# Last cross-attention of a decoder: exponentials meet context rows with a column of ones instead of projected values

## The chip, the cores and the metric

The kernel runs on one core of one Trainium2 chip, as one program. The time is device microseconds of one execution; lower is better. All arithmetic of the part discussed here is in float32.

## The reference

The program is a decoder of four layers, each with a self-attention, a cross-attention to a context of 1601 rows and a feed-forward part. After each part the input is added and a layer norm follows. x has the shape (4, 256, 128), the context (4, 1601, 96). The change concerns the last cross-attention alone:

```
def _L3_xattn_ref(x, context, Wq, Wk, Wv, Wo, bo):   # 16 heads of 64
    q = (x @ Wq).reshape(b, n, h, d).transpose(0, 2, 1, 3)
    k = (context @ Wk).reshape(b, -1, h, d).transpose(0, 2, 1, 3)
    v = (context @ Wv).reshape(b, -1, h, d).transpose(0, 2, 1, 3)
    sim = jnp.einsum('bhid,bhjd->bhij', q, k) * scale
    attn = jax.nn.softmax(sim, axis=-1)
    out = jnp.einsum('bhij,bhjd->bhid', attn, v)
    out = out.transpose(0, 2, 1, 3).reshape(b, n, h * d)
    return out @ Wo + bo
```

What follows it is a layer norm, an int8 feed-forward part and a last layer norm.

## The kernel before

The function `l3_xattn` (from line 1852) works through 32 units: a batch row b of 4 and a pair of heads hp of 8. The 1601 context rows of a unit are cut into 13 chunks of 128 rows (the last has 65), and these are worked on in four steps: four chunks in each of the first three, one in the fourth. The two heads of a pair lie in the two halves of 64 partitions. Scores are held transposed: context rows on the partitions, the 256 queries of each head along the free dimension. A tile `St` holds two chunks of both heads (128 x 1024).

TensorE (PE), VectorE (DVE) and ScalarE (ACT) each do their instructions in the order in which the code writes them (`manual_schedule`, line 2047); SyncE's loads and GpSimd's few instructions are placed by the framework. The loop at line 2048 counts steps g and writes for each:

- `running(g-1)` (DVE): the running maximum over the copied scores, L1937 and L1940; at a unit's end L1944 folds it to `mx`. For the first two steps of a unit's four it stands at the loop's top, for the others after the maxima.
- `spread` (PE, then an ACT copy to `Mb`, L1968): brings a unit's maxima to all partitions. Once per unit, where g % 4 is 1.
- `shifted(gb)` (DVE, L1974): subtracts the maxima from `St`. gb is g - 5: this half of the pipeline runs five steps, a little over a unit, behind the scores.
- `queries` (PE, DVE copy), once per unit, where g % 4 is 3.
- `projections(g+1, gb)`: PE makes the keys of step g+1 and the values of step gb in one PSUM tile of the pool `big`; ACT copies both halves out (L1918).
- `weights(gb)` (ACT, L1981): exponentials in place in `St`.
- `advance(later)`: lets deferred work take one step. Among it is `ended(u)`, which finishes a unit: two products spread the row sums, DVE takes the reciprocal (L2022) and multiplies (L2025).
- `sums(gb-1)` (PE): exponentials times values, and exponentials times a block of ones for the row sums, accumulated in one PSUM tile `acc` of the pool `one` over the unit's four steps. After the fourth, ACT copies the row sums to `rows` (L2013), and `ended` is put off to the next step.
- `maxima` (PE, DVE reduction L1956), once per unit, where g % 4 is 0.
- `scores(g)` (PE; ACT copies to `St`, L1930).

Values are projected per chunk with the context as stationary operand:

```
self.mm(ps[d, 512 + c * P : 512 + (c + 1) * P],
        self.ctx_all[:CD, o + d.start : o + d.stop], wv[:, hp * P : (hp + 1) * P])
```

An instruction of PE issued by the helper `mm` carries line 388 whatever it does, so the rows are told apart by their tiles. In the profile `big<-ctx,w` is the key projection, `big<-w,ctx` the value projection, `big<-Q,K` the scores, `one<-St,V` exponentials with values, `one<-St,c` exponentials with ones, `one<-rows,c` the products in `ended`, `one<-c,mx` the maxima and `one<-c,mq` the spread. A float32 product shows as two records. The shapes after a name are contraction rows x columns of the stationary operand, then rows x columns of the moving one.

PSUM has three tiles of the pool `big` (1024 columns) and two of the pool `one` (512 columns) in this stage. `acc` holds one of the two `one` tiles for most of a unit; queries, maxima and spread share the other.

Below, the four steps of a unit in the steady state are called A (g % 4 = 1, with the spread), B (2, with `ended` of the unit whose last chunk was summed in A), C (3, with the queries) and D (0, with the maxima).

Of the kernel before, what the change touches and what calls it, by code (L numbers as in the profile page):

```python
# [21 lines left out]
B, T, D = 4, 256, 128  # L22
P = 128
# [21 lines left out]
SW = 32  # L45
# [229 lines left out]
def _host(w):  # L275

    packs = {"c": _constants(), "p0": _pack0(w), "p1": _pack1(w), "p2": _pack2(w)}
    for i in range(NL):
        packs[f"p3_{i}"] = _pack3(w, i)
    packs["al"] = _alibi()  # L280
    packs["p4"], packs["p5"] = _pack4(w), _pack5(w)
    up, gp, down = Pack(NE * FM), Pack(NE * FM), Pack(sum(map(len, MOE_IN)) * D)
    up.add("w", w["L2_ffn_up_w"].transpose(2, 0, 1).reshape(D, NE * FM))
    gp.add("w", w["L2_ffn_gp_w"].transpose(2, 0, 1).reshape(D, NE * FM))
    dw = w["L2_ffn_down_w"].transpose(0, 2, 1)
    parts = []
    for e in range(NE):
        for i in MOE_IN[e]:
            parts.append(np.zeros((P, D), np.float32))
            lo, hi = max(MOE[i][0], e * FM), min(MOE[i][1], (e + 1) * FM)  # L290
            parts[-1][lo - MOE[i][0] : hi - MOE[i][0]] = dw[e, lo - e * FM : hi - e * FM]
    down.add("w", np.concatenate(parts, 1))
    packs.update(up=up, gp=gp, down=down)
    arrays = {n: c.a for n, c in packs.items()}
    ctx = w["ctx_768"].transpose(2, 0, 1).reshape(CD, B * S2)
    arrays["ctx"] = np.ascontiguousarray(ctx)
    arrays["x"] = np.ascontiguousarray(w["x"])
    arrays["mask"] = np.ascontiguousarray(w["mask_BxS2_bf1"]).view(np.uint8)
    arrays["wq8"] = np.ascontiguousarray(w["L3_ffn_weight_q"].T).view(np.int32)
    return arrays, {n: c.at for n, c in packs.items()}  # L300


class Net:
# [1548 lines left out]
    def l3_xattn(self):  # L1852
# [2 lines left out]

        nc = self.nc
        HD, LAG = 64, 5
        halves = [slice(0, HD), slice(HD, P)]  # L1860
        wq, wk, wv = self.w("p4", "Wq"), self.w("p4", "Wk", CD), self.w("p4", "Wv", CD)
        units = [(b, hp) for b in range(B) for hp in range(NH // 2)]
        steps = 4 * len(units)
        qs, ks, vs, sts, mx, top, accs, outs = {}, {}, {}, {}, {}, {}, {}, {}
        later = [self.in_turn(self.taken_over())]
        w8 = self.tile("w8", [P, D // 4], I32, pool=self.const)
        nc.sync.dma_start(w8, self.dram["wq8"])
# [3 lines left out]
        one = [kept[:, i].rearrange("p (n d) -> p n d", n=NB) for i in range(8, 11)]  # L1871
        places = {"h": kept[:, 4:8], "x1": one[0], "x3": one[1], "xn": one[2]}
        self.late = places.get

        def parts(g):

# [9 lines left out]
            qs[u] = self.tile("Q", [P, T], bufs=2)  # L1886
            nc.vector.tensor_copy(qs[u], ps[:, :T])

        def projections(gk, gv):

            ps, copies = self.big(), []
            if 0 <= gk < steps:
                b, hp = units[gk // 4]
                lo = gk % 4 * 4 * P
                n = min(4 * P, S2 - lo)
                for d in halves:
                    cols = slice(hp * P + d.start, hp * P + d.stop)
                    self.mm(ps[d, :n], wk[:, cols], self.ctx[:CD, b, lo : lo + n])
                ks[gk] = self.tile("K", [P, 4 * P], bufs=2)
                copies.append((ks[gk][:, :n], ps[:, :n]))  # L1900
            if 0 <= gv < steps:
                b, hp = units[gv // 4]
                lo = b * S2 + gv % 4 * 4 * P
                n = min(4, NCH - gv % 4 * 4)
                for c in range(n):
                    o = lo + c * P
                    for d in halves:
                        self.mm(
                            ps[d, 512 + c * P : 512 + (c + 1) * P],
                            self.ctx_all[:CD, o + d.start : o + d.stop],  # L1910
                            wv[:, hp * P : (hp + 1) * P],
                        )
                vs[gv] = self.tile("V", [P, 4, P], bufs=3)
                copies.append(
                    (vs[gv][:, :n, :].rearrange("p c d -> p (c d)"), ps[:, 512 : 512 + n * P])
                )
            for to, at in copies:
                nc.scalar.copy(to, at)  # L1918

        def scores(g):  # L1920
            u = g // 4
# [10 lines left out]
        def running(g):  # L1932
            u = g // 4
            for k, nc_, kp in parts(g):
                if k == 1:
                    mx[u] = kept[:, :4].rearrange("p (h c) t -> p h c t", h=2)
                    nc.vector.tensor_max(mx[u], sts[u, 0], sts[u, 1])  # L1937
                elif k:
                    to = mx[u][:kp, :, :nc_, :]
                    nc.vector.tensor_max(to, to, sts[u, k][:kp, :, :nc_, :])  # L1940
            if g % 4 == 3:
                m = mx.pop(u)
                mx[u] = self.tile("mx", [P, 2, T], bufs=2)
                nc.vector.tensor_max(mx[u], m[:, :, 0, :], m[:, :, 1, :])  # L1944

        def maxima(u):
# [11 lines left out]
        def spread(u):  # L1958

            ps, m = self.misc(), mx.pop(u)  # L1960
            for j in range(2 * NB):
                for d in halves:
                    self.mm(
                        ps[d, j * P : (j + 1) * P],
                        m[:, j : j + 1].broadcast_to([P, HD]), self.ident,
                    )
            top[u] = self.tile("Mb", [P, 2, T], bufs=2)
            nc.scalar.copy(top[u].rearrange("p h t -> p (h t)"), ps)  # L1968

        def shifted(g):  # L1970
# [12 lines left out]
        def sums(g):  # L1983
            u = g // 4
            if g % 4 == 0:
                accs[u] = self.misc()
            acc = accs[u]
            es = [(k, nc_, sts.pop((u, k))[:kp]) for k, nc_, kp in parts(g)]
            for k, nc_, e in es:
                for c in range(nc_):  # L1990
                    i = 2 * k + c
                    for h, d in enumerate(halves):
                        if i < NCH - 1:
                            self.mm(
                                acc[d, :T], vs[g][:, i - g % 4 * 4, d], e[:, h, c, :],
                                start=i == 0, stop=False,
                            )
            for k, nc_, e in es:
                kp = e.shape[0]
                for c in range(nc_):  # L2000
                    for h in range(2):
                        d = slice(HD * h + SW * c, HD * h + SW * c + SW)
                        self.mm(
                            acc[d, T:], self.w("c", "ones", kp)[:, :SW], e[:, h, c, :],
                            start=False, stop=False,
                        )
                if kp < P:
                    for h, d in enumerate(halves):
                        self.mm(acc[d, :T], vs[g][:kp, 0, d], e[:, h, 0, :], start=False)
            vs.pop(g)  # L2010
            if g % 4 == 3:
                rows = self.tile("rows", [P, T], bufs=1)
                nc.scalar.copy(rows, acc[:, T:])  # L2013
                later.append(ended(u, rows))

        def ended(u, rows):
            b, hp = units[u]
            acc = accs.pop(u)
            for d in halves:
                self.mm(acc[d, T:], self.w("c", "both")[:, d], rows)  # L2020
            rec = self.tile("rec64", [P, T])
            nc.vector.reciprocal(rec, acc[:, T:])  # L2022
            if hp == 0:
                outs[b] = self.tile(f"w{SLOT['p3_2']}", [P, NH // 2, T], pool=self.wpool)
# [20 lines left out]

        engines = {nc.tensor.engine, nc.vector.engine, nc.scalar.engine}
        with self.tc.manual_schedule(engines=engines):
            for g in range(-1, steps + LAG + 2):
                gb = g - LAG
                if g % 4 < 2 and 0 <= g - 1 < steps:  # L2050
                    running(g - 1)
                if g % 4 == 1 and 4 < g <= steps + 1:
                    spread(g // 4 - 1)
                if 0 <= gb < steps:
                    shifted(gb)
                if 0 <= g + 1 < steps and (g + 1) % 4 == 0:
                    queries((g + 1) // 4)
                if g + 1 < steps or gb < steps:
                    projections(g + 1, gb)
                if 0 <= gb < steps:  # L2060
                    weights(gb)
                self.advance(later)
                if 0 <= gb - 1 < steps:
                    sums(gb - 1)
                if g % 4 == 0 and 4 <= g <= steps:
                    maxima(g // 4 - 1)
                if g % 4 > 1 and 0 <= g - 1 < steps:
                    running(g - 1)
                if 0 <= g < steps:
                    scores(g)  # L2070
            while later:
                self.advance(later)
# [59 lines left out]
```

## Time and profile before

| | |
|---|---|
| Median of 3 runs | 2832.32 us (2829.03 to 2837.85) |
| Profiled execution | 2829.03 us, span 2827.2 us |
| PE busy | 2696.4 us (95% of the span) |
| PE weight loads busy | 1776.1 us (63%) |
| DVE busy | 1803.9 us (64%) |
| ACT busy | 1533.0 us (54%) |
| GpSimd (POOL) busy | 178.4 us (6%) |
| Mean granted clock of PE | 0.983 |
| The last attention with what follows | from 1957 to 2827.2 us, PE busy 845.91 of 870.20 us |

Engines have a queue each and wait for one another by semaphores. Time is in microseconds from the span's start; a timeline row gives the start, the length from the first start to the last end of a merged group, the engine, the line, the operation, the tiles written and read, the shapes and the number of records; a bracket holds the idle time ahead of it and who ended it. Matmuls overlap, so what one group costs is read from its start to the next group's start. Short idle times of the weight loader marked "issue" are not waits for another engine.

### The profile page before, as it was taken

Reading aid. Unit: us, or ns where it says so; the run is one execution under the profiler, and the core shown is the slowest. Engines: PE = TensorE matmul, PEld = TensorE weight load, DVE = VectorE, ACT = ScalarE, POOL = GpSimd, SP = SyncE. Lnnn points to the kernel's source line nnn. Section 1 sums busy time; section 2 is a strip of 40 time slices with the busy share of each in tenths; the row PEclk is TensorE's granted clock in tenths of the full one; section 3 lists DMA queues with packets and bytes.
Section 4 is the critical chain, followed back from the end, with each engine's and each line's share of the span. In section 5 each row is a group of like instructions: output and inputs, shape, how many; then the busy total and the mean of one; then the engine's idle time right before and its main releaser. Section 6 shows DMA issues by size and latency. Waiting matters only on the chain.

```text
span 2827.2 us, 62963 instructions
## 1 busy us (share of the span) xinstructions
PE 2696.4 (95%) x27003; PEld 1776.1 (63%) x27003; DVE 1803.9 (64%) x3946; ACT 1533.0 (54%) x2943; POOL 178.4 (6%) x191
## 2 busy tenths in 40 slices
PE   7999999898889999999999999998999999999997
PEld 4555565566655555555897777776656666666664
DVE  6656666364567665664455766665757777777775
ACT  2555555455534555555553444445656666666564
POOL 2000110110010000000001111101100000000000
PEclk9999999999989999999999999999999999999999
DMA  3000000000020000000002000000000000000000
GB/s 114 1 2 1 2 1 2 1 1 1 1 79 23 1 2 1 1 2 1 1 1 103 2 14 2 2 2 2 2 1 2 3 2 2 3 1 2 3 1 3
DMA packets 5223, 27.65 MB, mean 10 GB/s; under 512 B 584, under 2 KB 2764, under 8 KB 3408
## 3 DMA queue, kind: packets, MB, share of 16 engines
q1 hardware_dynamic: 4944, 23.62, 2.4%
q8 instruction: 212, 3.47, 0.5%
q14 instruction: 67, 0.55, 0.1%
HBM read 23.07 MB, written 0.52 MB: 8 GB/s over the span
## 4 chain that ended last, share of the span: by engine, by line
PE 87%; DVE 8%; ACT 2%; issue 1%; DMA 0%; POOL 0%; POOLq 0%; ACTq 0%; DVEq 0%; SPq 0%
PE one L388 63%; PE big L388 13%; PE acc L388 8%; DVE M L898 1%; PE one L533 1%; PE one L824 1%; PE one L461 1%; DVE St L1974 1%; DVE mpad L686 1%; DVE Ms L681 1%; ACT w L1313 0%; ACT E L720 0%; PE one L1323 0%; DVE w L1940 0%; DVE ln_st L475 0%
## 5 line engine op out<-in xcount | busy, mean ns | idle before, releaser
L898 DVE TENSOR_REDUCE M<-one 128x1 f32<-128x458 f32 (+3 forms) x1024 | 528.7, 568 | 292.2 <-PE one L388 291.0
L921 ACT ACTIVATE E<-one 128x512 f32<-128x512 f32 (+1 forms) x896 | 457.8, 563 | 424.0 <-PE one L388 423.7
L388 PE MATMUL one<-Q,K 32*128 32x256 f32 (+1 forms) x3328 | 532.8, 403 | 1.5 <-DVE M L898 1.5
L388 PE MATMUL one<-K,Q 32*128 32x458 f32 (+3 forms) x2048 | 459.2, 541 | 1.6 <-DVE M L898 1.6
L388 PEld LDWEIGHTS one<-Q,K 32*128 32x128 f32 (+1 forms) x3328 | 311.1, 180 | 62.4 <-DVE M L898 35.6
L1930 ACT COPY St<-big 128x1024 f32<-128x1024 f32 (+1 forms) x224 | 204.3, 959 | 159.8 <-PE big L388 159.8
L388 PEld LDWEIGHTS one<-K,Q 32*128 32x128 f32 x2048 | 171.3, 185 | 142.9 <-issue 79.9
L1974 DVE TENSOR_TENSOR St<-St,Mb 128x1024 f32<-128x1024 f32 (+1 forms) x224 | 245.3, 1142 | 1.8 <-ACT Mb L1968 1.8
L388 PE MATMUL acc<-E,V 128*32 128x256 f32 (+1 forms) x3328 | 234.1, 388 | 7.1 <-ACT E L921 7.1
L720 ACT ACTIVATE E<-one 128x384 f32<-128x384 f32 (+1 forms) x352 | 154.3, 525 | 143.9 <-PE one L388 143.7
L1981 ACT ACTIVATE St<-St 128x1024 f32<-128x1024 f32 (+1 forms) x224 | 215.1, 1014 | 25.4 <-DVE St L1974 25.3
L388 PE MATMUL big<-Q,K 64*128 64x256 f32 (+1 forms) x1664 | 214.4, 393 | 0.0
L388 PE MATMUL one<-St,V 128*64 128x256 f32 (+1 forms) x1664 | 204.1, 382 | 0.4
L481 POOL TENSOR_TENSOR ln_r<-ln_ve,half 128x2 f32<-128x2 f32 x92 | 71.0, 771 | 2104.5 <-DVE ln_ve L479 2047.0
L1940 DVE TENSOR_TENSOR w<-w,St 128x1024 f32<-128x1024 f32 (+1 forms) x160 | 178.7, 1117 | 34.7 <-ACT St L1930 27.5
L388 PE MATMUL one<-xT,w 128*128 128x256 f32 (+1 forms) x664 | 169.7, 396 | 18.6 <-DVE Q L1116 8.3
L681 DVE TENSOR_REDUCE Ms<-one 128x3 f32<-128x384 f32 x256 | 130.4, 552 | 84.8 <-PE one L388 84.6
L388 PEld LDWEIGHTS big<-Q,K 64*128 64x128 f32 (+1 forms) x1664 | 147.7, 183 | 57.4 <-issue 40.2
L388 PEld LDWEIGHTS acc<-E,V 128*32 128x32 f32 (+1 forms) x3328 | 87.5, 109 | 125.6 <-issue 70.8
L388 PEld LDWEIGHTS one<-St,V 128*64 128x64 f32 (+1 forms) x1664 | 113.5, 137 | 62.7 <-issue 14.6
L388 PEld LDWEIGHTS big<-w,ctx 96*64 96x64 f32 x1664 | 97.1, 137 | 54.0 <-issue 53.9
L388 PEld LDWEIGHTS one<-xT,w 128*128 128x128 f32 (+1 forms) x664 | 96.5, 180 | 49.5 <-issue 15.6
(308 smaller groups left out, 3978.0 us busy)
## 6 DMA issues: line engine op xcount, KB each, us to landing
w<-in_p SPq DMA_DIRECT2D x4, 1483.0 KB, 10.3
ctx<-in_ctx SPq DMA_DIRECT2D x4, 600.4 KB, 13.5
w<-in_down SPq DMA_DIRECT2D x1, 2112.0 KB
w<-in_up SPq DMA_DIRECT2D x1, 1632.0 KB, 6.3
w<-in_gp SPq DMA_DIRECT2D x1, 1632.0 KB
w<-in_p SPq DMA_DIRECT2D x1, 1536.0 KB, 15.1
w<-in_p SPq DMA_DIRECT2D x1, 1413.0 KB, 12.2
w<-in_p SPq DMA_DIRECT2D x1, 1382.0 KB
```

The costliest lines, as they stand in the source:

```text
L388: self.nc.tensor.matmul(out, lhsT, rhs, start=start, stop=stop)
L461: self.nc.tensor.transpose(ps[:, n * P : (n + 1) * P], x[:, n, :], self.ident)
L481: nc.gpsimd.tensor_tensor(rstd, ve, self.half[:, :NB], ALU.pow)
L533: self.nc.tensor.transpose(ps[:rows, n * P : (n + 1) * P], m4[:, n, :rows], self.ident)
L681: nc.vector.reduce_max(out=m[:, j, :], in_=ps[:, : 3 * P].rearrange("p (s c) -> p s c", c=P), axis=AX.X,)
L720: nc.scalar.activation(es[t, j], ps[:, :w], AF.Exp, scale=scale)
L898: nc.vector.reduce_max(out=ms[i][:, n, j, part : part + 1], in_=ps[:, at : at + hi - lo], axis=AX.X)
L921: nc.scalar.activation(e[:kp, :w], ps[:kp, :w], AF.Exp, scale=scale)
L1930: nc.scalar.copy(st[:kp, :, :nc_, :], ps[:kp, :, :nc_, :])
L1940: nc.vector.tensor_max(to, to, sts[u, k][:kp, :, :nc_, :])
L1974: nc.vector.tensor_sub(e, e, top[u][:kp].unsqueeze(2).broadcast_to([kp, 2, nc_, T]))
L1981: nc.scalar.activation(e, e, AF.Exp, scale=HD**-0.5)
```

## The change

The values are no longer projected. Each head's output is exp(S) (C Wv) / sum; the changed kernel computes (exp(S) C) Wv / sum.

- The host lays out the context rows a second time, with chunk rows on the partitions, padded to 13 chunks and with a 97th column of ones: the input `ctx_rows`. `context_rows(b)` loads one batch row of it (128 x 1261 float32, two buffers): b = 0 ahead of the loop, each further one in the step where g % 32 is 16.
- `projections` becomes `keys`: only the key projection and its one ACT copy are left.
- `sums` makes one product per chunk: the stationary operand is the chunk's 97 columns of context and ones, the moving operand the exponentials of both heads (512 columns), accumulated to a 97 x 512 tile. Rows 0 to 95 hold exp(S) C, row 96 the row sums. After the fourth step ACT copies all of it to `met`, where it copied 256 columns of row sums to `rows`.
- `ended` takes a second PSUM tile of the pool `one`: two products of the value weights of each head with `met` give the numerators, two of `last` (97 x 64, zeros but for ones in the last row) with `met` spread the row sums; reciprocal and multiplication stay.
- `mx`, `Mb` and `rec64` get one buffer instead of two. `last` is filled by two memsets of GpSimd.

```diff
+        def context_rows(b):
+            rows[b] = self.tile("rows", [P, NCH, CR], bufs=2)
+            n = NCH * CR
+            nc.sync.dma_start(
+                rows[b].rearrange("p c d -> p (c d)"),
+                self.dram["ctx_rows"][:, b * n : (b + 1) * n],
+            )
...
-        def projections(gk, gv):
...
+        def keys(g):
+            ps = self.big()
+            b, hp = units[g // 4]
+            lo = g % 4 * 4 * P
+            n = min(4 * P, S2 - lo)
+            for d in halves:
+                cols = slice(hp * P + d.start, hp * P + d.stop)
+                self.mm(ps[d, :n], wk[:, cols], self.ctx[:CD, b, lo : lo + n])
+            ks[g] = self.tile("K", [P, 4 * P], bufs=2)
+            nc.scalar.copy(ks[g][:, :n], ps[:, :n])
...
             if g % 4 == 0:
-                accs[u] = self.misc()
-            acc = accs[u]
...
+                accs[u] = self.misc()[:CR]
+            acc = accs[u].rearrange("p (h t) -> p h t", h=2)
+            for k, nc_, kp in parts(g):
+                e = sts.pop((u, k))
                 for c in range(nc_):
                     i = 2 * k + c
...
+                    self.mm(
+                        acc, rows[units[u][0]][:kp, i, :], e[:kp, :, c, :],
+                        start=i == 0, stop=i == NCH - 1,
+                    )
...
             if g % 4 == 3:
-                rows = self.tile("rows", [P, T], bufs=1)
-                nc.scalar.copy(rows, acc[:, T:])
-                later.append(ended(u, rows))
+                met = self.tile("met", [CR, 2, T], bufs=1)
+                nc.scalar.copy(met.rearrange("p h t -> p (h t)"), accs.pop(u))
+                later.append(ended(u, met))
...
-            acc = accs.pop(u)
-            for d in halves:
-                self.mm(acc[d, T:], self.w("c", "both")[:, d], rows)
+            acc = self.misc()
+            for h, d in enumerate(halves):
+                self.mm(acc[d, :T], wv[:, hp * P + d.start : hp * P + d.stop], met[:CD, h, :])
+            for h, d in enumerate(halves):
+                self.mm(acc[d, T:], last, met[:, h, :])
...
-                if g + 1 < steps or gb < steps:
-                    projections(g + 1, gb)
+                if 0 <= g + 1 < steps:
+                    keys(g + 1)
+                if g % 32 == 16 and 1 <= g // 32 + 1 < B:
+                    context_rows(g // 32 + 1)
```

More of the change, by code (lines that the diff above doesn't have):

```diff
@@ L296, in _host @@
     arrays["ctx"] = np.ascontiguousarray(ctx)
+    rows = np.zeros((B, NCH * P, CD + 1), np.float32)
+    rows[:, :S2, :CD] = w["ctx_768"]
+    rows[:, :S2, CD] = 1.0
+    rows = rows.reshape(B, NCH, P, CD + 1).transpose(2, 0, 1, 3)
+    arrays["ctx_rows"] = np.ascontiguousarray(rows.reshape(P, B * NCH * (CD + 1)))
     arrays["x"] = np.ascontiguousarray(w["x"])
@@ L1859, in l3_xattn @@
         HD, LAG = 64, 5
+        CR = CD + 1
         halves = [slice(0, HD), slice(HD, P)]
@@ L1863, in l3_xattn @@
         steps = 4 * len(units)
-        qs, ks, vs, sts, mx, top, accs, outs = {}, {}, {}, {}, {}, {}, {}, {}
+        qs, ks, rows, sts, mx, top, accs, outs = {}, {}, {}, {}, {}, {}, {}, {}
         later = [self.in_turn(self.taken_over())]
@@ L1873, in l3_xattn @@
         self.late = places.get
+        last = self.tile("last", [CR, HD], bufs=1)
+        nc.gpsimd.memset(last, 0.0)
+        nc.gpsimd.memset(last[CD:], 1.0)
+        def context_rows(b):
[5 more added lines that the diff above has]
+            )
         def parts(g):
@@ L1887, in queries @@
             nc.vector.tensor_copy(qs[u], ps[:, :T])
-        def projections(gk, gv):
[L1891 to L1895, printed above, removed]
-                for d in halves:
[L1897 to L1918, printed above, removed]
+        def keys(g):
[8 more added lines that the diff above has]
+            nc.scalar.copy(ks[g][:, :n], ps[:, :n])
         def scores(g):
@@ L1942, in running @@
                 m = mx.pop(u)
-                mx[u] = self.tile("mx", [P, 2, T], bufs=2)
+                mx[u] = self.tile("mx", [P, 2, T], bufs=1)
                 nc.vector.tensor_max(mx[u], m[:, :, 0, :], m[:, :, 1, :])
@@ L1966, in spread @@
                     )
-            top[u] = self.tile("Mb", [P, 2, T], bufs=2)
+            top[u] = self.tile("Mb", [P, 2, T], bufs=1)
             nc.scalar.copy(top[u].rearrange("p h t -> p (h t)"), ps)
@@ L1985, in sums @@
             if g % 4 == 0:
-                accs[u] = self.misc()
-            acc = accs[u]
-            es = [(k, nc_, sts.pop((u, k))[:kp]) for k, nc_, kp in parts(g)]
-            for k, nc_, e in es:
+                accs[u] = self.misc()[:CR]
+            acc = accs[u].rearrange("p (h t) -> p h t", h=2)
+            for k, nc_, kp in parts(g):
+                e = sts.pop((u, k))
                 for c in range(nc_):
                     i = 2 * k + c
[L1992 to L2009, printed above, removed]
@@ L2010, in sums @@
-            vs.pop(g)
+                    self.mm(
+                        acc, rows[units[u][0]][:kp, i, :], e[:kp, :, c, :],
+                        start=i == 0, stop=i == NCH - 1,
+                    )
             if g % 4 == 3:
-                rows = self.tile("rows", [P, T], bufs=1)
-                nc.scalar.copy(rows, acc[:, T:])
-                later.append(ended(u, rows))
-        def ended(u, rows):
+                met = self.tile("met", [CR, 2, T], bufs=1)
+                nc.scalar.copy(met.rearrange("p h t -> p (h t)"), accs.pop(u))
@@ L2017, in ended @@
+                later.append(ended(u, met))
+        def ended(u, met):
             b, hp = units[u]
-            acc = accs.pop(u)
-            for d in halves:
-                self.mm(acc[d, T:], self.w("c", "both")[:, d], rows)
-            rec = self.tile("rec64", [P, T])
+            acc = self.misc()
[3 more added lines that the diff above has]
+                self.mm(acc[d, T:], last, met[:, h, :])
+            rec = self.tile("rec64", [P, T], bufs=1)
@@ L2047, in l3_xattn @@
         with self.tc.manual_schedule(engines=engines):
+            context_rows(0)
             for g in range(-1, steps + LAG + 2):
```

## The prediction

> **What bounds the kernel now.** The change touches only the last attention, so I read the page's chain first, then busy time by stretch inside that stage, then the timeline of one unit (one batch row, two heads).
>
> ```profile
> PE 87%; DVE 8%; ACT 2%; issue 1%; DMA 0%; POOL 0%; POOLq 0%; ACTq 0%; DVEq 0%; SPq 0%
> ```
>
> ```profile
> 2300.00:2400.00 100.00, 100.00 (x1080) 63.02 (x1078) 71.77 (x72) 69.08 (x98) 0.00 (x0) 1.00 0.01 1
> ```
>
> The chain runs over PE, and in these 100 us PE is never idle at a granted clock of 1.00, while DVE (72) and ACT (69) have room. So a unit costs what PE's order of work costs, start to start. That is read from the timeline (start, length, engine, line); starts matter, lengths overlap:
>
> ```profile
> 2300.52 1.09 PE L388 MATMUL one<-c,mq 128*64 128x128 f32 x16
> ...
> 2301.79 1.23 DVE L1937 TENSOR_TENSOR w<-St,St 128x1024 f32<-128x1024 f32 x1 [2.38 <-ACT St L1930]
> ...
> 2302.93 4.62 DVE L1974 TENSOR_TENSOR St<-St,Mb 128x1024 f32<-128x1024 f32 x4
> ...
> 2304.42 2.00 PE L388 MATMUL big<-Q,K 64*128 64x256 f32 x16
> 2306.32 0.37 ACT L2013 COPY rows<-one 128x256 f32<-128x256 f32 x1
> ...
> 2306.34 0.34 PE L388 MATMUL big<-ctx,w 96*64 96x65 f32 x4
> ...
> 2306.51 1.04 PE L388 MATMUL big<-w,ctx 96*64 96x128 f32 x16
> ...
> 2307.39 0.60 PE L388 MATMUL one<-rows,c 128*64 128x256 f32 x4
> ...
> 2307.82 1.90 PE L388 MATMUL one<-St,V 128*64 128x256 f32 x16
> ...
> 2309.65 1.07 PE L388 MATMUL one<-St,c 128*32 128x256 f32 x16
> ...
> 2310.65 2.00 PE L388 MATMUL big<-Q,K 64*128 64x256 f32 x16
> ```
>
> The next unit's `c,mq` begins at 2325.11, so a unit is 24.59 us. Its four steps start at 2300.52, 2306.34, 2312.57 and 2318.20: A (spread) 5.82, B (`ended`) 6.23, C (queries) 5.63, D (maxima) 6.91. Note `rows`: ACT copies it at 2306.32, done by 2306.69; PE asks for it only at 2307.39, because 16 value-projection records lie ahead. At the end of the kernel, with less PE work ahead, the same place does stall (1.54 us, last line):
>
> ```profile
> 2787.78 4.63 DVE L1974 TENSOR_TENSOR St<-St,Mb 128x1024 f32<-128x1024 f32 x4 [1.81 <-ACT Mb L1968]
> ...
> 2791.14 0.35 ACT L2013 COPY rows<-one 128x256 f32<-128x256 f32 x1
> ...
> 2791.55 0.65 PE L388 MATMUL one<-rows,c 128*64 128x256 f32 x4 [1.54 <-ACT rows L2013]
> ```
>
> **PE work removed, per unit** (start to start). Value projections .97+.88+.87+.22 = 2.94. Exponentials with V: 3x1.83, and .58 for the 65-row chunk, 6.07. Row sums by ones: 3x1.00+.56 = 3.56. The two `both` products .43. Together 13.00. A float32 product is two records.
>
> **PE work added.** 13 products of 97 columns over 512 moving columns, and two pairs in `ended`. No row has this shape exactly; the nearest is a full-width product with 512 moving columns in an earlier stage:
>
> ```profile
> 616.01 1.02 PE L388 MATMUL one<-ctx,w 97*128 97x512 f32 x2
> 616.87 1.05 PE L388 MATMUL one<-w,ctx 97*128 97x128 f32 x8
> ```
>
> One product takes .86 start to start, so 13 are 11.1. The pairs, two halves side by side like `both`, are .43 each: .86. Bare sum 11.98 against 13.00: one microsecond gained. The 13 give no gain by themselves: V work ran two products side by side (8 in 1.83) and ones four (8 in 1.00), and a 97-column product has no neighbour. Bounds: .85 each (two in 1.71 at 626.34) up to 1.0, if operand strides between the heads cost something; I take .86.
>
> **Switches of shape.** The removed figures already contain what is lost between groups of different shape; the new .86 doesn't. The start of this stage shows full-width products among half-width ones:
>
> ```profile
> 1957.79 1.06 PE L388 MATMUL big<-ctx,w 96*64 96x512 f32 x4
> 1958.78 0.44 PE L461 MATMUL one<-c,heads 128*128 128x128 f32 x2
> 1959.14 1.08 PE L388 MATMUL big<-ctx,w 96*64 96x512 f32 x4
> 1960.15 0.71 PE L388 MATMUL one<-w,oT 128*128 128x128 f32 x4
> 1960.80 1.57 PE L388 MATMUL big<-Q,K 64*128 64x256 f32 x12
> ```
>
> Keys into full width: .99 and 1.01 where keys followed by value projections take .86, so +.15. Full width into scores: .65 for 4 records of 128 columns that need .43, so +.21. The Trainium skill ("TensorEngine Tiling (Array Packing)", Key Properties) says that changing the tiling mode, not just the tile, drains the engine. Counting modes by that rule, B and C keep three switches, D four and A goes from four to three: by the rule's count the drains nearly cancel and about 1 us per unit stays won. The rows differ: V to ones lost .12 and ones to scores .15, while the new pair costs .15+.21. I take the rows, which decide.
>
> So, without waits: A: spread .93, keys 1.01, one product .86+.21, scores 1.92 = 4.93. B: keys .17, `ended` .86+.13, four products 3.42+.21, scores 1.92 = 6.71. C: queries .49, keys 1.01, 3.63, scores .58 = 5.71. D: keys 1.01, 3.62, maxima 1.02, scores 1.93 = 7.58. Sum 24.93 against 24.59: +.34 per unit before any wait.
>
> **The wait that appears.** Now `ended` needs `met`, a copy of the accumulator by ACT, queued behind two exponentials of the same step. Those follow DVE: scores of D, their copies, L1937, then the subtractions L1974. None of this chain is shortened. ACT loses its V copy ahead of the exponentials (.60), but the first must then wait for the first subtraction and the second for the second. The stage's end shows that case: first subtraction 2787.78 to `both` 2791.55 is 3.77 us. `met` (97x512) costs .59 by the 128x512 row of `Mb` (.586) instead of .35, so 4.01. In the steady unit the subtraction starts 2.41 after the spread (2302.93-2300.52), so `ended` starts at 6.42. PE arrives at 4.93+.17 = 5.10 and waits 1.32. Behind it on PE queue the step's four products and scores B; ACT's copies and DVE's maxima wait for those. In exchange nothing comes earlier: the loop's start is scores of D, which move with PE. New period: 6.42 + .99+3.63+1.92 (rest of B) + 5.71 + 7.58 = 26.25, or +1.66 per unit.
>
> **What is covered.** ACT is relieved of 2.07 us of V copies a unit and pays .22 for `met`; it is not the bound, so nothing is gained. `mx`, `Mb`, `rec64` with one buffer: each is last read over 5 us before its rewrite a unit later. Four DMAs of 646 KB (128 x 1261 x 4 bytes; 13.5 us to land for `ctx`, 600 KB): the first is needed six steps in, some 25 us later, the others about 16 steps after issue; SP has only outputs to pass. Were the first late, PE would wait at most those 13.5 us once. The two POOL memsets are needed some 45 us in, after queued POOL work of .7 to 1.6 us a piece. Extra PSUM tile in `ended`: freed after the multiplication (2309.90+.42 = 9.8 after the spread), wanted by queries at 6.42+.99+3.63+1.92 = 12.96; cost nothing, up to 1 us if that cover went.
>
> **Sum.** 30 units have both the wait and followers: 30x1.66 = 49.8. The first units carry leftover work of the stage before, which fills some wait: about -3 (estimate: one step of .4 to 2 us in each of four units). The first unit has no `ended`: -.3. At the end the last `met` comes about 1.4 later (2803.31 to 2804.75 by the same durations). Together +48 on the profiled execution's 2829.0, its span 2827.2 and 1.8 around it: 2877. The median stands 3.3 above that execution; I forecast 2878, 1.6% slower.
>
> **Rivals.** (1) Wait without switch costs: .86 everywhere, bare PE sum 23.6, `ended` still at 6.42; period 6.42+.86+3.44+1.92+5.37+7.29 = 25.30, +.71, 2829+21 = 2851. For it: the rule's count. Against: the rows at 1958 to 1960.
> (2) Only switches, no wait: +.34 x 31 = 11, 2841. It asks that `met` is ready at 5.1; against it, two exponentials behind two subtractions.
> (3) Faster: the fewer, longer products run without drains and without the wait, -.97 x 31 = -30, 2800. One mechanism, PE's freed microsecond staying free; it needs `ended` ready at step B's start. With switches free, the period falls below 24.59 once `met` is ready before 5.71 (6.42 less .71). For it: PE is the bound and instructions fall from 80 to 17 products per unit. Against: the 1.54 stall above.
> (4) Worse: the 97-column product over two strided halves runs at 1.0 instead of .86: 12 of them outside the wait add 1.7 a unit, 2930. For it only that no row has the stride.
>
> **How the numbers follow.** Likeliest .66 (2864 to 2892: .3 a switch or half a microsecond of wait either way), rival 1 .12, rival 2 .08 (half of it near no change), rival 3 .07, rival 4 .07. Range 2842 to 2900: it leaves out rivals 3 and 4 and the lower half of 2, .18 in all. A difference under .3% (8.5 us) can't be told from none by a measurement of this kernel. Faster .07, same .05, slower .88; low-lying rival 2 counts in the last two.
>
> **What would show it.** The `ended` products should start with an idle time of about 1.3 us put down to the copy of `met`; four 512-column products should stand 3.4 to 3.7 us ahead of scores; spreads 26.2 us apart; DVE and ACT no busier. PE without idle time there, or products at other than .86, would prove the prediction wrong. The granted clock shouldn't move: gaps of 1.54 us left it at 1.00 in the stage's end (2786 to 2803).

## The result, and the profile after

The changed kernel takes 2874.99 us (median of 4 runs, 2872.47 to 2875.76), the kernel before 2833.89 (4 runs, 2829.03 to 2837.85). The ratio is 1.0144, with a 95% interval of 1.0126 to 1.0162: slower by 1.4%. The forecast was 2878, within 2842 to 2900. The profiled execution took 2872.47 us, its span is 2870.7, which is 43.5 more than before.

First the chain of the changed kernel, by engine and by line (helper lines have moved by five, so PE's products carry L393):

```profile
PE 86%; DVE 8%; ACT 3%; issue 2%; DMA 0%; POOL 0%; ACTq 0%; POOLq 0%; DVEq 0%; SPq 0%
PE one L393 65%; PE big L393 10%; PE acc L393 8%; DVE M L903 1%; PE one L538 1%; PE one L829 1%; DVE St L1973 1%; PE one L466 1%; DVE mpad L691 1%; ACT met L1997 1%; DVE Ms L686 1%; ACT w L1318 0%; PE one L1328 0%; ACT E L725 0%; DVE ln_st L480 0%
```

The copy to `met` (ACT, L1997) is on the chain now; the copy to `rows` was not. Busy time by engine (PE, weight loads, DVE, ACT, POOL), granted clock and DMA, in 100 us of the steady stage:

```profile
2300.00:2400.00 100.00, 95.20 (x527) 45.01 (x526) 67.36 (x69) 60.16 (x79) 0.00 (x0) 1.00 0.00 1
```

PE halved its instructions (1080 to 527) and is idle 4.8 us where it had no idle time; DVE and ACT are less busy than before. The waits from 2080 to 2786 us name the cause (who waited for whom, us in total, times, longest):

```profile
PE one L393 <- ACT met L1997: 28.2, 26, 1.2
```

The timeline of one steady unit shows the place:

```profile
2312.09 1.09 PE L393 MATMUL one<-c,mq 128*64 128x128 f32 x16
...
2313.98 1.10 PE L393 MATMUL one<-St,rows 65*97 65x512 f32 x2
...
2314.51 4.62 DVE L1973 TENSOR_TENSOR St<-St,Mb 128x1024 f32<-128x1024 f32 x4
...
2315.01 2.00 PE L393 MATMUL big<-Q,K 64*128 64x256 f32 x16
2315.76 2.19 ACT L1980 ACTIVATE St<-St 128x1024 f32<-128x1024 f32 x2 [1.02 <-DVE St L1973]
...
2316.94 0.34 PE L393 MATMUL big<-ctx,w 96*64 96x65 f32 x4
2317.86 0.57 ACT L1997 COPY met<-one 97x512 f32<-97x512 f32 x1
...
2318.47 0.65 PE L393 MATMUL one<-met,w 96*64 96x256 f32 x4 [1.20 <-ACT met L1997]
...
2319.49 3.67 PE L393 MATMUL one<-St,rows 128*97 128x512 f32 x8
...
2323.10 2.00 PE L393 MATMUL big<-Q,K 64*128 64x256 f32 x16
```

The accumulator is complete about 2315 us. Its copy starts at 2317.86, behind the two exponentials (2315.76, 2.19 long), the first of which waited for the first subtraction. PE has nothing to do for 1.20 us. The next spread starts at 2338.22, so a unit takes 26.13 us instead of 24.59.

From the first spread to the last the stage takes 847.6 us (1976.8 to 2824.43) instead of 808.7 (1977.3 to 2786.03): +38.9. From the last spread to the end it takes 46.2 instead of 41.2: +5.0.

### The profile page after: what moved, and what is told of

It reads as the page before. It is cut to its first block, busy times and chain, and to the rows that moved or that the text cites. A ratio compares the mean times of both kernels' runs of the same rounds, so it can differ in the third digit from the quotient of the medians.

```text
span 2870.7 us, 54722 instructions
## 1 busy us (share of the span) xinstructions
PE 2701.3 (94%) x22971; PEld 1659.8 (58%) x22971; DVE 1802.8 (63%) x3946; ACT 1493.4 (52%) x2815; POOL 178.4 (6%) x193
## 4 chain that ended last, share of the span: by engine, by line
PE 86%; DVE 8%; ACT 3%; issue 2%; DMA 0%; POOL 0%; ACTq 0%; POOLq 0%; DVEq 0%; SPq 0%
PE one L393 65%; PE big L393 10%; PE acc L393 8%; DVE M L903 1%; PE one L538 1%; PE one L829 1%; DVE St L1973 1%; PE one L466 1%; DVE mpad L691 1%; ACT met L1997 1%; DVE Ms L686 1%; ACT w L1318 0%; PE one L1328 0%; ACT E L725 0%; DVE ln_st L480 0%
## 5 line engine op out<-in xcount | busy, mean ns | idle before, releaser
L393 PE MATMUL one<-Q,K 32*128 32x256 f32 (+1 forms) x3328 | 533.1, 404 | 1.5 <-DVE M L903 1.5
L393 PE MATMUL one<-K,Q 32*128 32x458 f32 (+3 forms) x2048 | 459.4, 541 | 1.6 <-DVE M L903 1.6
L393 PE MATMUL one<-St,rows 128*97 128x512 f32 (+1 forms) x832 | 389.5, 607 | 0.0
L393 PEld LDWEIGHTS one<-Q,K 32*128 32x128 f32 (+1 forms) x3328 | 311.6, 180 | 62.1 <-DVE M L903 35.5
L393 PEld LDWEIGHTS one<-St,rows 128*97 128x97 f32 (+1 forms) x832 | 127.6, 165 | 232.3 <-issue 169.0
L393 PEld LDWEIGHTS one<-K,Q 32*128 32x128 f32 x2048 | 171.9, 186 | 142.8 <-issue 80.2
L393 PE MATMUL acc<-E,V 128*32 128x256 f32 (+1 forms) x3328 | 234.1, 388 | 7.0 <-ACT E L926 7.0
L393 PE MATMUL big<-Q,K 64*128 64x256 f32 (+1 forms) x1664 | 214.5, 393 | 0.0
L393 PEld LDWEIGHTS big<-Q,K 64*128 64x128 f32 (+1 forms) x1664 | 147.8, 184 | 93.5 <-issue 35.3
L393 PE MATMUL one<-xT,w 128*128 128x256 f32 (+1 forms) x664 | 170.6, 398 | 18.6 <-DVE Q L1121 8.3
L393 PEld LDWEIGHTS acc<-E,V 128*32 128x32 f32 (+1 forms) x3328 | 87.6, 109 | 125.5 <-issue 70.8
L393 PEld LDWEIGHTS one<-xT,w 128*128 128x128 f32 (+1 forms) x664 | 97.0, 181 | 50.0 <-issue 15.6
L393 PE MATMUL one<-Ks,Q 32*128 32x256 f32 (+1 forms) x1408 | 106.2, 375 | 19.0 <-ACT E L725 9.0
```

The source lines that it names most:

```text
L393: self.nc.tensor.matmul(out, lhsT, rhs, start=start, stop=stop)
```

## Experiments

Each is an edit of the changed kernel, but for the fifth. Unit lengths are from one spread to the next in a stretch like the one above.

**The wait taken away.** In step A the copy to `met` goes ahead of the two exponentials in ACT's queue. PE's order stays.

```diff
-                if 0 <= gb < steps:
+                if 0 <= gb < steps and g % 4 != 1:
                     weights(gb)
                 self.advance(later)
                 if 0 <= gb - 1 < steps:
                     sums(gb - 1)
+                if 0 <= gb < steps and g % 4 == 1:
+                    weights(gb)
```

> The changed kernel with one edit: in the step that sums a unit's last chunk (A), the copy to met is written ahead of the two exponentials in ACT's queue instead of behind them. PE's order is untouched. Theory (the wait for met behind two exponentials costs 1.20 us a unit, as the profile after shows): met is ready before PE asks, the idle time of the met products vanishes, spreads stand 24.8 us apart instead of 26.13, and the time falls from 2875 by some 30 x 1.3 to about 2836 to 2843, a little above the kernel before. Rival (changes of shape on PE alone make the loss): nothing moves, 2875. Rival (the wait alone makes the loss and the products are a gain of a microsecond): below the kernel before by some 25, about 2808.

Measured: 2832.07 us (14 runs), ratio to before 1.0002 (0.9994 to 1.0011): no difference from the kernel before, and a little below the 2836 to 2843 expected. The timeline of the unit:

```profile
2304.33 1.09 PE L393 MATMUL one<-c,mq 128*64 128x128 f32 x16
...
2309.17 0.34 PE L393 MATMUL big<-ctx,w 96*64 96x65 f32 x4
2309.33 0.60 PE L393 MATMUL one<-met,w 96*64 96x256 f32 x4
2309.77 0.60 PE L393 MATMUL one<-met,last 97*64 97x256 f32 x4
2310.30 3.67 PE L393 MATMUL one<-St,rows 128*97 128x512 f32 x8
...
2329.03 1.09 PE L393 MATMUL one<-c,mq 128*64 128x128 f32 x16
```

The idle time ahead of `met,w` is gone, and a unit takes 24.70 us: 1.43 less than in the changed kernel, .11 more than before the change. Of the 1.43, 1.20 is the idle time; the rest is that products following without a gap start sooner after one another (keys to `met,w` .16, `met,w` to `met,last` .44; with the wait, .33 of keys ahead of it and .49). So in the steady units the wait makes nearly all of the loss.

The edit moves one more thing. `advance` too now stands ahead of the exponentials in step A, and with it, in the first batch row, an activation left over from the stage before (ACT, L1776 in the kernel before, L1781 in the others), for which PE waits once. That wait in the kernel before, in the changed kernel and in this experiment:

```profile
2062.45 2.08 PE L388 MATMUL one<-xnT,w 128*128 128x256 f32 x4 [4.22 <-ACT w L1776]
2062.81 2.08 PE L393 MATMUL one<-xnT,w 128*128 128x256 f32 x4 [5.04 <-ACT w L1781]
2066.87 1.13 PE L393 MATMUL one<-xnT,w 128*128 128x256 f32 x4 [1.82 <-ACT w L1781]
```

With 10.2, 10.2 and 3.4 us at half clock around it, the time from the fourth spread to the fifth is 38.19, 38.41 and 32.47 us. So some 6 of the 43 us that the edit gains have nothing to do with `met`. Without them it would stand at about 2838 us (an estimate from these lengths), within what was expected. The wait for `met` then makes some 37 of the 41 us of the loss; the products and changes of shape by themselves cost the few us that remain, which the gain in the first batch row hides here. Neither rival held.

**The wait made longer.** The copy is made twice, then three times.

```diff
+                nc.scalar.copy(met.rearrange("p h t -> p (h t)"), accs[u])
                 nc.scalar.copy(met.rearrange("p h t -> p (h t)"), accs.pop(u))
```

> The changed kernel with the copy to met done twice in a row, the same data to the same place. Theory (met is on the path one for one): PE's idle time ahead of the met products grows by about .48 us, one copy start to start, and so does every unit; 30 units give +14, about 2889. Rival (the wait has slack, or changes of shape make the loss): no change, 2875, since ACT has 40% idle time.

Measured: 2911.1 us (4 runs), 36 above the changed kernel and not 14. The idle time grew to 1.82, by .62 and not by .48 (the second copy starts .60 after the first), and a unit without a disturbance to 26.74 (2301.03 to 2327.77), +.61. The rest is the clock. Between the first spread and the last the granted clock fell in ten places, besides the one between the fourth spread and the fifth, where it falls in the changed kernel too. This is one of them, behind a wait of 1.82; first the timeline, then busy times and clock (the third figure from the end) around it:

```profile
2185.60 0.34 PE L393 MATMUL big<-ctx,w 96*64 96x65 f32 x4
2187.76 0.92 PE L393 MATMUL one<-met,w 96*64 96x256 f32 x4 [1.82 <-ACT met L1998]
2188.46 1.07 PE L393 MATMUL one<-met,last 97*64 97x256 f32 x4
2189.46 4.63 PE L393 MATMUL one<-St,rows 128*97 128x512 f32 x8
```

```profile
2184.00:2188.00 4.00, 2.18 (x22) 1.55 (x20) 3.79 (x4) 3.47 (x5) 0.00 (x0) 1.00 0.00 0
2188.00:2191.00 3.00, 3.00 (x10) 1.16 (x7) 1.43 (x1) 3.00 (x5) 0.00 (x0) 0.50 0.00 0
2191.00:2195.00 4.00, 4.00 (x17) 1.78 (x17) 3.86 (x5) 0.55 (x1) 0.00 (x0) 0.95 0.00 0
```

For about 3.4 us PE runs at half clock, and the four products take 4.63 where they take 3.67 elsewhere. A stretch costs half of its 3.4 us; ten make 17 us. With .61 x 30 = 18 that is 35 of the 36.

> The changed kernel with the copy to met three times over. PE's idle time grows from 1.82 (two copies) to about 2.3 us, which by itself is +.48 a unit, +14 over the 2911 of e2_met_twice. In e2_met_twice nine stretches of 3.4 us at half clock followed waits of 1.82, in the changed kernel with waits of 1.20 none did in the steady units. If the chance of such a stretch grows with the length of the wait: more than nine, each costing 1.7 us, 2930 to 2950. If it is a matter of chance and not of the wait: about nine again, 2925.

Measured: 2958.47 us (2 runs), above the expected range. The wait is 2.44 us:

```profile
2315.54 0.65 PE L393 MATMUL one<-met,w 96*64 96x256 f32 x4 [2.44 <-ACT met L1999]
```

The clock fell in nineteen places from 2080 to 2896 us, mean 0.95 (0.98 with two copies, 1.00 with one), and in six of them for 6.8 us instead of 3.4, which the expectation had not counted. Not every fall follows a wait of the full length, as the expectation has it: three of the nineteen, and three of the nine with two copies, stand at the end of a batch row, where an idle time of .79 us and a shorter wait for `met` (1.43, and .82 with two copies) come close together. By single waits: of 25 of 1.20 us none was followed by half clock, of 24 of 1.82 us seven, of 25 of 2.44 us seventeen. The last section says what tells them apart.

**Fewer changes of shape.** In both of these the copy to `met` stays ahead. First, the keys of both heads become one product of 128 columns:

```diff
-            for d in halves:
-                cols = slice(hp * P + d.start, hp * P + d.stop)
-                self.mm(ps[d, :n], wk[:, cols], self.ctx[:CD, b, lo : lo + n])
+            self.mm(ps[:, :n], wk[:, hp * P : (hp + 1) * P], self.ctx[:CD, b, lo : lo + n])
```

> As e1_met_first, and the key projection of both heads is one product of 128 columns instead of two of 64 side by side, so that keys and sums have one shape. Theory (a change of shape costs .10 to .15): keys to the first of the sums fall from .96 to .86 in A, C and D, step B gains a change between keys and ended; net -.15 to -.3 a unit, 5 to 9 us below e1_met_first. If changes of shape cost nothing: the same time as e1_met_first.

Measured: 2838.12 us (14 runs), ratio to before 1.0019 (1.0007 to 1.0030). The expectation failed even in its sign: 6 us above the first experiment. Timeline of step A:

```profile
2308.56 1.09 PE L393 MATMUL one<-c,mq 128*64 128x128 f32 x16
2309.59 1.13 PE L393 MATMUL big<-ctx,w 96*128 96x512 f32 x2
2310.55 1.02 PE L393 MATMUL one<-St,rows 65*97 65x512 f32 x2
2311.50 2.00 PE L393 MATMUL big<-Q,K 64*128 64x256 f32 x16
2313.43 0.44 PE L393 MATMUL big<-ctx,w 96*128 96x65 f32 x2
2313.80 0.65 PE L393 MATMUL one<-met,w 96*64 96x256 f32 x4
```

I had counted the change taken away behind the keys, and not the one put in ahead of them: the spread in front is half width. Spread to keys is 1.03 (it was .92), keys to the sum is .96 as before, and in step B the 65-column keys now take .37 instead of .16. Over a unit there are thirteen changes as in the first experiment, and it takes 24.88 us instead of 24.70.

Second, queries, maxima and spread become full width too, and `ended` goes ahead of the keys in step B:

```diff
-                    for d in halves:
-                        cols = slice(n * P + d.start, n * P + d.stop)
-                        self.mm(ps[d, o : o + P], m[:, h, cols], self.ident)
+                    self.mm(ps[:, o : o + P], m[:, h, n * P : (n + 1) * P], self.ident)
...
+                if g % 4 == 2:
+                    self.advance(later)
                 if 0 <= g + 1 < steps and (g + 1) % 4 == 0:
                     queries((g + 1) // 4)
...
-                self.advance(later)
+                if g % 4 != 2:
+                    self.advance(later)
```

> As e3_keys_wide, and queries, maxima and spread are full-width products too (half as many, each twice as wide), and ended comes ahead of the keys in step B. Changes of shape per unit fall from 13 to 9. Theory: -.1 to -.2 for each of the four, 24.0 to 24.4 us a unit, 12 to 25 us below e1_met_first and so at or below the kernel before, about 2815 to 2830. If changes of shape cost nothing: the same as e1_met_first.

Measured: 2821.39 us (5 runs), ratio to before 0.9961 (0.9948 to 0.9974): faster than both kernels. The unit:

```profile
2301.99 0.65 PE L393 MATMUL one<-met,w 96*64 96x256 f32 x4
...
2308.76 0.70 PE L393 MATMUL one<-xT,w 128*128 128x256 f32 x2
2309.30 1.02 PE L393 MATMUL big<-ctx,w 96*128 96x512 f32 x2
2310.16 3.60 PE L393 MATMUL one<-St,rows 128*97 128x512 f32 x8
...
2326.31 0.65 PE L393 MATMUL one<-met,w 96*64 96x256 f32 x4
```

Keys between full-width neighbours take .86, and a unit 24.32 (2301.99 to 2326.31), .38 less than in the first experiment with four changes fewer. The edits are not told apart among themselves. Of the 11 us to the kernel before, 4.4 come from the first batch row as in the first experiment (33.79 us from the fourth spread to the fifth, for 38.19); an order of ACT's work that spares this wait was not tried in the kernel before.

Fifth, the control: the kernel before with the same four groups at full width. The edit of the queries stands for all:

```diff
-            for d in halves:
-                self.mm(ps[d, :T], wq[:, hp * P + d.start : hp * P + d.stop], self.xT[b])
+            self.mm(ps[:, :T], wq[:, hp * P : (hp + 1) * P], self.xT[b])
```

> The kernel before with keys, queries, maxima and spread as full-width products, as in e4_all_wide, and nothing else. Theory (the gain of e4_all_wide over e1_met_first, .38 us a unit, is fewer changes of shape, and depends on the sums being full-width too): here the values and the row sums stay half and quarter width, changes of shape rise from 14 to 18 a unit, so +.3 to +.6 a unit, 9 to 19 us slower than before, about 2842 to 2851. Rival (full-width products are cheaper by themselves, whatever stands beside them): some 10 us faster than before, 2822.

Measured: 2856.33 us (4 runs), ratio 1.0081 (1.0058 to 1.0104), 24 us slower and more than expected. Every step gained length: A 6.04 from spread to keys (it was 5.82), C 5.83 (5.63), D 7.17 (6.91), with B at 6.48 (6.23), keys to scores 4.55 and the scores' 1.93 from the unit ahead. A unit takes 25.51 us, .92 more, for four more changes. So full width is no gain in itself; beside half-width groups it is a loss. A price for a change of shape can't be given either: .10 each in one kernel, .23 in the other.

**Is it the missing neighbour?** On the first experiment, each product of the sums takes only 64 context columns, and even and odd chunks go to opposite halves. Context columns 64 to 95, the row sums and the adding of the halves are left out.

```diff
+                    d = halves[i % 2]
                     self.mm(
-                        acc, rows[units[u][0]][:kp, i, :], e[:kp, :, c, :],
-                        start=i == 0, stop=i == NCH - 1,
+                        acc[d], rows[units[u][0]][:kp, i, :HD], e[:kp, :, c, :],
+                        start=i < 2, stop=i >= NCH - 2,
                     )
```

> As e1_met_first, but each product of sums takes only the first 64 columns of its context chunk, and even and odd chunks go to opposite halves of the columns. It leaves out context columns 64 to 95, the row sums and the adding of the two halves, so it shows time alone. Theory (a 97-column product costs what two half-width ones cost side by side, because it has no neighbour): the products pair up, four of a step take about 1.9 us instead of 3.6, a unit loses some 5 us of PE and then waits for other engines, about 2690. Rival (a product costs by its 512 moving columns, neighbour or not): no change, 2832.

Measured: 2765.58 us (2 runs), ratio 0.9765 (0.9738 to 0.9791). Timeline of the steps B and D:

```profile
2308.21 1.89 PE L393 MATMUL one<-St,rows 128*64 128x512 f32 x8
2310.03 2.00 PE L393 MATMUL big<-Q,K 64*128 64x256 f32 x16
...
2316.61 1.89 PE L393 MATMUL one<-St,rows 128*64 128x512 f32 x8
2320.57 1.09 PE L393 MATMUL one<-c,mx 128*64 128x128 f32 x16 [2.08 <-DVE mx L1943]
```

Four products take 1.82 start to start where 97 columns take 3.61, so two of them do run side by side (in the trace the records of a pair start 7 ns apart). The time fell less than expected: PE then waits for DVE's maxima (2.08 in the last line; 49.5 us in 25 waits from 2080 to 2700), and the clock falls after such waits (mean 0.96 from 2080 to 2726).

## Why the prediction was right

**The wait.** Predicted: PE at `ended` 5.10 us after the spread, `met` ready at 6.42, a wait of 1.32. Measured: 5.18 (2318.47 less 1.20 less 2312.09), 6.38, 1.20. The bound read from the end of the kernel before (first subtraction to `both`, with a longer copy) gave this to within .04. The first experiment shows that the wait is some nine tenths of the loss.

**PE's work.** Predicted for the rest of B, then C and D: 6.54, 5.71, 7.58. Measured: 6.55 (2318.47 to 2325.02), 5.63 (2325.02 to 2330.65), 7.57 (2330.65 to 2338.22). The 97-column product costs .86, as the full-width row said, and the stride between the heads costs nothing: rival 4 falls. The added changes of shape were taken a little high: keys to sum .96 for 1.01 in A and C (in D it is 1.01), sum to scores 1.03 for 1.07. A unit without the wait was to cost +.34 and costs +.11 (first experiment), with the wait +1.66 and costs +1.54.

**The rule and the rows.** By the count of mode changes (the Trainium skill, "TensorEngine Tiling (Array Packing)", Key Properties) the first experiment would have ended at about 23.6 us a unit, some 30 us below the kernel before. It ended at 24.70. The rows were the better guide: the changes are thirteen where there were fourteen, but the time lost at them differs from pair to pair (.10 from keys to sum, .17 from the sum to scores), and the rule gives no price.

**The rivals.** 1 (wait without changes of shape, 2851) and 2 (no wait, 2841) fall with the first experiment and the waits. 3 (faster, 2800) needed both costs to be nothing; with the wait removed the time is that of before. But a gain is within reach: with the wait gone, fewer changes of shape and the shorter wait in the first batch row the algorithm does beat the kernel before, by 0.4%.

**Two terms of the sum were mis-sized, with opposite signs.** That they partly cancel is luck. The units: predicted 49.8 less 3.3, measured 38.9. Even 30 x 1.54 is 46. The first four periods grew by 1.1 together, where three of them with an `ended` would have given 4.6: the leftover work of the stage before fills part of the waits, as said. Units at the end of a batch row also grow less, for example from 34.28 to 35.59 us and the one after it from 25.66 to 26.40; this I had not counted. The end of the kernel: predicted +1.4, measured +5.0. The step that failed is "gaps of 1.54 us left it at 1.00": without the value projections the gap there is longer than the old one. Timeline, then busy times and clock (third figure from the end) of the changed kernel:

```profile
2830.17 1.12 PE L393 MATMUL one<-met,w 96*64 96x256 f32 x4 [3.61 <-ACT met L1997]
...
2832.07 13.56 PE L393 MATMUL one<-St,rows 128*97 128x512 f32 x26
```

```profile
2826.00:2830.00 4.00, 0.56 (x2) 0.00 (x0) 3.81 (x4) 2.63 (x4) 0.00 (x0) 0.95 0.00 0
2830.00:2836.00 6.00, 5.83 (x13) 2.32 (x14) 4.60 (x5) 2.44 (x4) 0.00 (x0) 0.50 0.00 0
```

The clock fell at the end of a wait of 3.61 us and stayed at half for 6.8 us (its length in the trace's clock record), which costs 3.4 of the missing 3.6. With `met` copied first it does not fall there: the same 26 records take 11.40 us instead of 13.56, and the two groups ahead of them lose less too.

**What was covered stayed covered.** The context rows landed in 3.7 us (median), and PE waited for no DMA in the stage.

## What to carry to other kernels

Fewer and wider products are not less PE time where the narrow ones ran side by side: compare the time from group to group, not the number of instructions. Work that is removed ahead of a consumer also removes the cover of a copy, so look in the other engine's queue for what that copy stands behind; here moving one copy ahead of two exponentials gave back some nine tenths of the loss. When an edit moves a whole stretch of a queue, look for what else moved with it. When the shapes of neighbouring groups are changed, look at both sides of each group, and don't take the count for the price: with thirteen changes a unit took 24.70 us in one arrangement and 24.88 in another.

## What the hardware showed unexpectedly

Short waits of PE can bring the granted clock down to half, and more of them the longer they are: none of 25 at 1.20 us, seven of 24 at 1.82, seventeen of 25 at 2.44, each time for 3.4 or 6.8 us. Two copies more on an engine with 40% idle time cost 83 us of the kernel's 2875, about 44 of them by the clock (99 us at half clock between the first spread and the last, where the changed kernel has 10).

The clock records of the traces show what tells one wait from another. In each trace all changes of the clock fall on a grid of 3.413 us. For each stretch of this grid at full clock, from the first spread to the last and over the nine traces, PE's idle time within it was added up. Under 1.6 us (2037 stretches) the next stretch was never at half clock; from 1.6 to 1.86 us (29 stretches) it was 20 times; above that (37 stretches) always. So a wait of 1.82 us can count where it lies within one stretch, and not where the grid cuts it into two short parts; a wait of 1.20 us alone cannot. With three copies, seven waits of 2.44 us in a row (2288 to 2452) passed without a fall: units of 27.36 us are nearly eight lengths of the grid (27.31), so the grid cut each of them at nearly the same place, with 1.80 down to 1.48 us in one stretch. This was read from the traces afterwards and no run was made to test it; it holds for this stage, and in earlier stages, with products of other shapes, the clock also fell after less idle time than that.
